# A graph layer on one core: who copies the products of picked rows, and where three steps stand in the order

## The chip, the core and the metric

The kernel runs on one core of a Trainium2 chip. The core has a matrix engine (PE; its weight loads are listed as PEld), a vector engine (DVE), a scalar engine (ACT), GpSimd (POOL), which here issues the gathers from memory, and SyncE (SP), which here issues ordinary DMAs. Each engine works through its own instruction list in order, and semaphores tie the lists together. The metric is the device time of one execution in microseconds. Three runs of the kernel before took 5995.97, 5999.37 and 6003.86 us, median 5999.37.

## The reference

One graph layer on 12500 nodes of 128 features and 412500 edges sorted by destination, then a residual sum and a layer norm:

```
f0, f1   = linear(x)                      # per node: 32 scalars, 32 three-vectors
h        = gelu(gelu(ea8 @ Wm1) @ Wm2)    # per edge, 64 wide
w00, w01, w10, w11 = h @ Wp_..            # per edge, 4 x 32 weights
mid      = products of w.., ea4 and f0[src], f1[src]
n        = segment_sum(mid, dst)          # over the edges of a node
y        = cos * self(x) + sin * linear(n)
out      = layernorm(x + y)
```

The awkward part is `f[src]`: for each of the 412500 edges a row of 128 numbers has to be brought from the node `src`, which is anywhere.

## The kernel before, in words

Edges are taken in runs of 512 (4 columns of 128 edges). Two runs are a pair, two pairs are a chunk. There are 806 runs, 403 pairs and 202 chunks. A pair with k = 0 is the first of its chunk, k = 1 the second. At the start the node features are turned and kept in SBUF (`xT`, feature by node), multiplied by `wf`, and written to a table in memory, 25 groups of up to 512 nodes.

The main loop goes over pairs `p`. The gathered rows of a pair lie in a buffer `GP[p]` (10 buffers of two runs). A column of 128 rows gets there in one of three ways:

- an indirect DMA from POOL reads 128 rows of the table (`gather`, line 223);
- 128 single-row DMAs from SP (`aid`, line 208), for one column of every fourteenth run;
- picking: ACT or DVE copies 128 single columns of `xT`, each at an address loaded into a register (`fetch`, line 174; `copy_columns`, line 188 on DVE and 192 on ACT), into a tile `gt`; when it is full, `picked_rows` multiplies it with `wf` on PE (line 197) into a PSUM tile `h`, and ACT copies the product to its place in `GP` (line 198). `SLOTS` says how many columns each engine copies at each of its places in a pair.

A column that is picked or aided needs no indirect DMA. The lists `picked` follow from `SLOTS`: with the sizes of before DVE picks 132 columns a chunk (64 and 68) and ACT 112 (56 and 56), and a product falls due wherever 128 are full; that makes 203 products on DVE, 171 on ACT, 2794 gathers. The product of a run is made two pairs before the pair that uses it.

For each pair the engines do, in this order:

- PE: `segments(p-1)` (line 670), the products of picked rows (197), `radial` (543, k = 1), `weights(p+1)` (597), `mlp1` (554, k = 0) or `mlp2` (570, k = 1) of the chunk two ahead, and at k = 0, last, `place(c-1)` (693 and 697), which moves the sums of the chunk before into a window of the bank `m`.
- ACT: `segments_kept` (676), picks, the copies of the products (198), picks, the two gelus (559 at k = 0, 576 at k = 1), each followed by picks, and at k = 0 `show` (632) between the gelus, which writes to the same bank `m`.
- DVE: at k = 0 `placing` (683) and `hot_rows` (624); then the three parts of `messages` (650, 654, 654) with picks between; at k = 1 also `select` (639), which reads what `show` wrote in the bank, and `add` (710), which adds the placed window to the sums.
- POOL: the gathers for the pair nine ahead, into the buffer that `messages(p-1)` has just finished reading.

A pick group on ACT that comes with an operation loads half of its addresses, does the operation, copies these columns, then loads and copies the other half. The PSUM tiles named `h` have two buffers, which products, `radial`, `mlp1` and `mlp2` share in the order of the program. Every eighth chunk or so a group of 512 nodes is finished: `moments` on PE, a copy and a move of the sums on ACT (741, 428), statistics on DVE.

The order is written out by hand; the framework puts in the semaphore waits. A tile's readers wait for all its writers, the bank `m` and a pair's buffer counted as one tile.

Of the kernel before, what the change touches and what calls it, by code (L numbers as in the profile page):

```python
# [8 lines left out]
F32 = mybir.dt.float32  # L9
# [3 lines left out]
AF = mybir.ActivationFunctionType  # L13
OP = mybir.AluOpType
PE = mybir.EngineType.PE
ACT = mybir.EngineType.Activation
# [5 lines left out]
P = 128  # L22
# [3 lines left out]
Q = 4  # L26
# [3 lines left out]
CH = 4  # L30
# [15 lines left out]
AID_FROM = 36  # L46
AID_LEAD = 16
STEPS = 12
SLOTS = {DVE: ((24, 20, 20), (24, 16, 28)), ACT: ((12, 16, 16, 12), (12, 16, 16, 12))}
FROM = {DVE: 6, ACT: 6}  # L50
COL_Q = {DVE: Q - 2, ACT: Q - 3}
A_OF = (1, 2, 3, 0)
# [5 lines left out]
def gnn_kernel(ctx: ExitStack, tc: tile.TileContext, x, src, dst, ea4, ea8, w1_0, w1_1, wm1, wm2,  # L58
# [120 lines left out]
    def copy_columns(e, columns):  # L179

        for at, r in columns:
# [9 lines left out]
            else:  # L191
                nc.scalar.activation(to, col, AF.Copy)  # L192

    def picked_rows(e, i):

        pt = ps.tile([P, P], F32, name="h")
        nc.tensor.matmul(pt, GT.pop((e, i)), wf, start=True, stop=True)  # L197
        nc.scalar.activation(G[picked[e][i]][:, COL_Q[e], :], pt, AF.Copy)  # L198

    def aid(s, t):  # L200

# [413 lines left out]
        nc.scalar.activation(G[s], pf, AF.Copy)  # L615

    OH = {}

    def hot_rows(c):

# [321 lines left out]
    with tc.manual_schedule(engines={PE, ACT, DVE, SP}):  # L942
        load_raw_rows(nc.sync, 0, min(3, raw_runs))
        load_w1(nc.scalar)
        if raw_runs > 3:
            load_raw_rows(nc.scalar, 3, raw_runs)
        for s in range(min(LEAD - 2, raw_runs)):
            gather(s)
        nc.vector.tensor_scalar(ident, diag, 0.0, None, op0=OP.is_equal)
        nc.vector.tensor_copy(none[:, :P], iota)  # L950
        nc.vector.tensor_copy(bank[:, 4 * SPAN:4 * SPAN + P // 2], none[:, :P].bitcast(F32))
        for b in range(min(3, NG)):
            XT[b] = load_nodes(b)
        make_wf()
        clear()
        loads = list(weight_loads())
        new_sums()
        extra = {2: lambda: load_edges(0), 3: lambda: load_attributes(0), NG // 2 - 2: lambda: turn_attributes(0), 4: lambda: load_raws(0), NG // 2: lambda: load_indices(0),
                 NG // 2 + 3: make_w1b, NG // 2 + 5: make_ws, NG - 6: lambda: radial(0), NG - 4: lambda: networks(0),
                 NG - 2: lambda: networks2(0), NG - 1: make_wpost,  # L960
                 NG // 2 + 1: lambda: nc.vector.memset(A["next"], 0.0),
                 NG - 3: run_places}
        for b in range(NG + 2):
            if b < NG:
                turn(b)
            if 0 < b <= NG:
                features_of(b - 1)
            if 1 < b:
                store_nodes(nc.scalar, table, b - 2, PF[b - 2])
            if b + 3 < NG:  # L970
                XT[b + 3] = load_nodes(b + 3)
            if b > 4 and loads:
                nc.sync.dma_start(*loads.pop(0))
            if b in extra:
                extra[b]()
        assert not loads
        for c in range(1, min(EDGES_AHEAD, NCH)):
            load_edges(c)
        if aided:
            aid_load()  # L980
        for s in range(min(LEAD - 2, raw_runs), min(LEAD, NS)):
            gather(s)
        for c in range(1, min(3, NCH)):
            radial(c)
            if c == 1:
                networks(c)
                networks2(c)
        weights(0)
        show(0)
        hot_rows(0)  # L990
        select(0)
        for s in range(PR):
            turn_rows(s)
        for s in range(PR):
            features(s)
        A["now"] = A["next"]
        clearing = []
        placed = added = 0

        def picks(e, p, i, op=None):  # L1000
            if p < FROM[e]:
                if op:
                    op()
                return
            n = SLOTS[e][p % (CH // PR)][i]
            if not op:
                copy_columns(e, fetch(e, n))
                return
            first = fetch(e, n // 8 * 4)
            op()  # L1010
            copy_columns(e, first + fetch(e, n - n // 8 * 4))

        for p in range(NP):
            c, k = divmod(p, CH // PR)
            mine = [s for s in range(p * PR, (p + 1) * PR) if s < NS]
            if p:
                for s in mine:
                    if s + LEAD - PR < NS:
                        gather(s + LEAD - PR)
            if k == 1 and c + EDGES_AHEAD < NCH:  # L1020
                load_edges(c + EDGES_AHEAD)
            for s in mine:
                if s % P == P // 2 - 16 and (s // P + 1) * P < NS:
                    load_raws(s // P + 1)
                if s % P == P // 2 and (s // P + 1) * P < NS:
                    load_indices(s // P + 1)
                if s % ET == 8 and s - 8 + ET < NS:
                    load_attributes(s // ET + 1)
                for t in range(P // ROWS):
                    a = s + AID_LEAD - t * STEPS // (P // ROWS)  # L1030
                    if a in aided:
                        aid(a, t)
            nets = c + 2 < NCH
            if k == 0:
                placing(c)
                if c + 1 < NCH:
                    hot_rows(c + 1)
            if p:
                segments(p - 1)
                picks(ACT, p, 0, lambda: segments_kept(p - 1))  # L1040
            for e in picked:
                for s in mine:
                    if (e, s + 2 * PR) in pick_of:
                        picked_rows(e, pick_of[e, s + 2 * PR])
            if k == 1 and c + 3 < NCH:
                radial(c + 3)
            cleared = bool(late)
            rest = list(kept)
            norm_kept()
            picks(ACT, p, 1)  # L1050
            if p + 1 < NP:
                weights(p + 1)
            if nets:
                (mlp1, mlp2)[k](c + 2)
                picks(ACT, p, 2, lambda: (gelu1, gelu2)[k](c + 2, 0))
            else:
                picks(ACT, p, 2)
            if k == 0 and c + 1 < NCH:
                show(c + 1)
            for s in mine:  # L1060
                if s % ET == 20 and s - 20 + ET < NS:
                    turn_attributes(s // ET + 1)
            if nets:
                picks(ACT, p, 3, lambda: (gelu1, gelu2)[k](c + 2, 1))
            else:
                picks(ACT, p, 3)
            if k == 0 and c > 0:
                place(c - 1)
                placed = c
            raws_next = [s + PR for s in mine if s + PR < raw_runs]  # L1070
            for s in raws_next:
                turn_rows(s)
            messages(p, 0)
            if k == 0:
                picks(DVE, p, 0)
            messages(p, 1)
            picks(DVE, p, 1 - k)
            for s in raws_next:
                features(s)
            if rest:  # L1080
                norm_rest()
            if cleared:
                new_sums()
                clearing += list(range(4))
            elif clearing:
                clear_sums(clearing.pop(0))
            if k == 1 and c + 1 < NCH:
                select(c + 1)
            if k == 1:
                picks(DVE, p, 1)  # L1090
            messages(p, 2)
            if k == 1 and placed > added:
                add(added)
                added += 1
            picks(DVE, p, 2)
            if k == 0 and 0 < added == c - 1:
                norm(due.get(added - 1, []))
            if p == 0:
                addresses()
                find_first()  # L1100
                new_sums()
                clearing = list(range(4))
            if p == NP - 4:
                count_odd()
        finish_waiting()
        segments(NP - 1)
        segments_kept(NP - 1)
        if late:
            norm_kept()
            new_sums()  # L1110
            clearing += list(range(4))
        norm_rest()
        finish_waiting()
        for i in clearing:
            clear_sums(i)
        for c in range(added, NCH):
            if c >= placed:
                place(c)
            add(c)
            if c < NCH - 1 and c in due:  # L1120
                norm(due[c])
                norm_kept()
                norm_rest()
                finish_waiting()
        norm_last(due[NCH - 1])
# [31 lines left out]
```

## Time and profile before

| what | value |
| --- | --- |
| median of three runs | 5999.37 us |
| profiled execution | 5962.68 us, span 5960.8 us |
| busy PE / DVE / ACT / POOL | 57% / 56% / 52% / 44% |
| granted clock of PE | 0.65 |
| indirect DMAs | 2722 from the table and 72 from x |
| column copies | 25984 on DVE (145 ns each), 21888 on ACT (189 ns each) |
| products copied by ACT | 374, 257 ns each |
| DMA | 239 MB, 40 GB/s |

Busy time counts what an engine executes; the stretch in which its sequencer loads registers, waits for semaphores or starts nothing is idle time. The column copies overlap their neighbours: a row of 16 takes 1.59 us on ACT, 20 take 1.30 us on DVE, so about 0.093 and 0.06 us each. In a timeline row the bracket at the end is the idle time of the engine just before, and who ended it; "issue" means that the profile shows no one.

### The profile page before, as it was taken

What the parts mean: (1) busy time and instruction counts of PE and PEld (TensorE: products, weight loads), DVE (VectorE), ACT (ScalarE), POOL (GpSimd) and SP (SyncE); (2) the same over time, 40 slices, a digit from 0 to 9 for tenths busy, and PEclk for the clock granted to TensorE, in tenths of its full rate; (3) what the DMA queues carried; (4) which work ended last, traced back from release to release, by engine and by line L of the source; (5) the groups of instructions that cost most, each with busy time, mean ns of one, the idle gap of its engine ahead of it and who ended that gap; (6) DMA issues with size and microseconds to landing.
All of it is one profiled execution on the core that took longest, in us unless ns stands there. A gap on an engine that the chain in (4) does not pass through costs nothing. (4 is left out here: it accounts for less than half of the span.)

```text
span 5960.8 us, 141936 instructions
## 1 busy us (share of the span) xinstructions
PE 3407.7 (57%) x30231; PEld 2603.1 (44%) x30231; DVE 3366.2 (56%) x28706; ACT 3093.4 (52%) x24111; POOL 2636.3 (44%) x2801
## 2 busy tenths in 40 slices
PE   3665655556555555555556555556655555655556
PEld 2544444444444444444444444444434444443444
DVE  1265656555655555656555665566565555665556
ACT  0254555555555555555555555555554555555554
POOL 4344444444444444444444444444444444444441
PEclk5766666666666666666666666666666666666666
DMA  4211111111111111111111111111111111111111
GB/s 100 59 36 40 39 35 38 41 35 43 42 35 39 39 37 43 40 35 36 36 41 37 40 43 38 37 40 40 41 40 35 35 38 38 40 40 34 40 33 23
DMA packets 576979, 239.04 MB, mean 40 GB/s; under 512 B 481402, under 2 KB 526570, under 8 KB 576106
## 3 DMA queue, kind: packets, MB, share of 16 engines
q0 software_dynamic: 89408, 183.29, 10.8%
q1 hardware_dynamic: 465928, 40.14, 5.4%
q10 hardware_dynamic: 20770, 6.47, 0.5%
q14 instruction: 629, 5.15, 0.3%
q8 instruction: 244, 4.00, 0.3%
HBM read 216.86 MB, written 12.99 MB: 39 GB/s over the span
## 5 line engine op out<-in xcount | busy, mean ns | idle before, releaser
L223 POOL DMA_INDIRECT G<-table,idx x2722 | 2567.2, 943 | 3208.9 <-issue 1313.3
L192 ACT ACTIVATE gt<-xT 128x1 f32 x21888 | 2329.1, 189 | 924.5 <-issue 889.3
L188 DVE COPY gt<-xT 128x1 f32 x25984 | 1891.8, 145 | 1565.0 <-issue 1520.5
L670 PE MATMUL seg<-M,S 128*32 128x128 f32 x12896 | 845.7, 371 | 444.2 <-issue 426.8
L597 PE MATMUL w<-wpb,h 64*128 64x128 f32 x6448 | 855.1, 388 | 383.7 <-issue 383.1
L597 PEld LDWEIGHTS w<-wpb,h 64*128 64x128 f32 x6448 | 699.0, 277 | 554.6 <-issue 544.1
L670 PEld LDWEIGHTS seg<-M,S 128*32 128x32 f32 x12896 | 544.3, 148 | 692.1 <-issue 643.3
L654 DVE TENSOR_TENSOR M<-w,G 128x768 f32<-128x768 f32 x806 | 761.1, 945 | 2.7 <-issue 2.7
L676 ACT ACTIVATE sg<-seg 128x256 f32<-128x256 f32 x403 | 151.1, 375 | 1112.3 <-remote 777.6
L697 PEld LDWEIGHTS m<-pl,sg 128*128 128x128 f32 x1612 | 348.6, 312 | 797.7 <-issue 797.7
L693 PE MATMUL m<-none 128*128 128x384 bf16 x202 | 90.8, 450 | 786.1 <-ACT m L632 412.6
L554 PE MATMUL h<-eT,w1b 64*128 64x128 f32 x3232 | 439.3, 403 | 125.8 <-ACT G L198 95.9
L576 ACT ACTIVATE h<-h 128x512 f32<-128x512 f32 x404 | 237.1, 589 | 491.9 <-remote 377.0
L554 PEld LDWEIGHTS h<-eT,w1b 64*128 64x128 f32 x3232 | 394.3, 303 | 159.5 <-ACT G L198 120.5
L570 PE MATMUL h<-h,w2b 64*64 64x256 f32 x3232 | 393.5, 556 | 105.7 <-ACT G L198 68.7
L197 PE MATMUL h<-wf,gt 128*128 128x128 f32 x748 | 244.0, 411 | 268.2 <-issue 154.2
L650 DVE TENSOR_TENSOR M<-w,G 128x512 f32<-128x512 f32 x403 | 275.5, 684 | 204.1 <-remote 73.9
L697 PE MATMUL m<-pl,sg 128*128 128x128 f32 x1612 | 367.5, 404 | 0.0
L197 PEld LDWEIGHTS h<-wf,gt 128*128 128x128 f32 x748 | 162.8, 263 | 403.6 <-issue 246.9
L639 DVE TENSOR_TENSOR S<-oh,m 128x512 f32<-128x512 f32 x202 | 137.2, 679 | 356.7 <-PE m L697 251.4
L559 ACT ACTIVATE h<-h 128x512 f32<-128x512 f32 x404 | 234.6, 581 | 91.0 <-remote 37.9
L570 PEld LDWEIGHTS h<-h,w2b 64*64 64x64 f32 x3232 | 187.5, 186 | 214.9 <-ACT G L198 87.3
(123 smaller groups left out, 1592.5 us busy)
## 6 DMA issues: line engine op xcount, KB each, us to landing
G<-table SPq DMA_DIRECT2D x7040, 0.5 KB
G<-table,idx POOLq DMA_INDIRECT x2722
e<-in_edge_attr SPq DMA_DIRECT2D x201, 64.0 KB
xt<-in_x SPq DMA_DIRECT2D x24, 256.0 KB
table<-ft ACTq DMA_DIRECT2D x24, 256.0 KB
xt<-in_edge_attr SPq DMA_DIRECT2D x24, 256.0 KB
out<-y SPq DMA_DIRECT2D x24, 256.0 KB
xt<-in_dst SPq DMA_DIRECT2D x5, 256.0 KB
```

Of the source, the lines that this page charges most:

```text
L188: nc.vector.tensor_copy(to, col)
L192: nc.scalar.activation(to, col, AF.Copy)
L197: nc.tensor.matmul(pt, GT.pop((e, i)), wf, start=True, stop=True)
L223: nc.gpsimd.indirect_dma_start(out=G[s][:, q, :], out_offset=None, in_=x if s < raw_runs else table, in_offset=bass.IndirectOffsetOnAxis(a ...
L554: nc.tensor.matmul(p1[h][:, j // 2, j % 2, :], w1b[rows, j, :], eT[c][rows, :], start=True, stop=True)
L570: nc.tensor.matmul(p2[r][k * HID:(k + 1) * HID, h * n:(h + 1) * n], w2b[rows, :], H1[c][h][rows, k * n:(k + 1) * n], start=True, stop=True)
L576: nc.scalar.activation(H2[c][r].rearrange("p k j e -> p (k j e)"), P2[c][r], AF.Gelu_apprx_tanh, scale=1.0 / math.sqrt(HID))
L597: nc.tensor.matmul(WP[p][:, i, q, :], H2[c][q % 2][rows, k, q // 2, :], wpb[rows, :], start=True, stop=True)
L650: nc.vector.tensor_tensor(m[:, :, :, :MUL], w[:, :, :2 * MUL].rearrange("p q (a u) -> p q a u", a=2), g[:, :, None, :MUL].to_broadcast([P, ...
L654: nc.vector.tensor_tensor(m[:, :, j, MUL:].rearrange("p q (i u) -> p q i u", i=3), w[:, :, None, (2 + j) * MUL:(3 + j) * MUL].to_broadcast ...
L670: nc.tensor.matmul(SEG[c][q * W:(q + 1) * W, r + i, :], own[:, (r + i) * Q + q, h * W:(h + 1) * W], M[p][:, i, q, h, :], start=h == 0, sto ...
L697: nc.tensor.matmul(to[:, :, bass.ds(k_at, 4 * W)].bitcast(F32), SG[c][:, k, :], PL[c][:, k, :].rearrange("p (a n) -> p a n", a=4), start=F ...
```

## The change

Five edits:

1. `SLOTS`: DVE copies 64 and 64 columns in the two pairs of a chunk (the last slot of the second goes from 28 to 24), ACT 64 and 64 (its first and last slots from 12 to 16). Every chunk then fills exactly one `gt` on each engine, with the last copy of its second pair, and both products fall due in the next pair with k = 0.
2. `picked_rows` only multiplies; a new `rows_kept` copies the product, on DVE instead of ACT, after the first part of `messages` (at k = 1 after the second).
3. `place(c-1)` stands on PE between `weights` and `mlp1`, and ahead of `show` in the program, instead of after the layer.
4. At k = 0, in nearly all chunks, DVE copies one number of each gathered row of the chunk's second pair to a small tile `landed` that nobody reads, so that it waits there for that pair's gathers.
5. The order of `messages` and the first picks is written differently; for k = 0 and k = 1 it comes out as before, but for the copies of the products.

```
-SLOTS = {DVE: ((24, 20, 20), (24, 16, 28)), ACT: ((12, 16, 16, 12), (12, 16, 16, 12))}
+SLOTS = {DVE: ((24, 20, 20), (24, 16, 24)), ACT: ((16, 16, 16, 16), (16, 16, 16, 16))}
...
+    PT = {}
+
     def picked_rows(e, i):
-        pt = ps.tile([P, P], F32, name="h")
+        PT[e, i] = pt = ps.tile([P, P], F32, name="h")
         nc.tensor.matmul(pt, GT.pop((e, i)), wf, start=True, stop=True)
-        nc.scalar.activation(G[picked[e][i]][:, COL_Q[e], :], pt, AF.Copy)
+
+    def rows_kept(e, i):
+        nc.vector.tensor_copy(G[picked[e][i]][:, COL_Q[e], :], PT.pop((e, i)))
...
+    landed = cst.tile([P, PR, Q], F32)
...
+            products = [(e, pick_of[e, s + 2 * PR]) for e in picked for s in mine if (e, s + 2 * PR) in pick_of]
+            for e, i in products:
+                picked_rows(e, i)
...
             if p + 1 < NP:
                 weights(p + 1)
+            if k == 0 and c > 0:
+                place(c - 1)
+                placed = c
             if nets:
                 (mlp1, mlp2)[k](c + 2)
...
-            if k == 0 and c > 0:
-                place(c - 1)
-                placed = c
             raws_next = [s + PR for s in mine if s + PR < raw_runs]
             for s in raws_next:
                 turn_rows(s)
+            if k == 0 and raw_runs <= PR * (p + 1) < NS - 6 * CH:
+                nc.vector.tensor_copy(landed, GP[p + 1][:, :, :, 0])
             messages(p, 0)
+            if k == 1:
+                messages(p, 1)
+            for e, i in products:
+                rows_kept(e, i)
+            picks(DVE, p, 0)
             if k == 0:
-                picks(DVE, p, 0)
-            messages(p, 1)
-            picks(DVE, p, 1 - k)
+                messages(p, 1)
+                picks(DVE, p, 1)
```

More of the change, by code (lines that the diff above doesn't have):

```diff
@@ L1040, in gnn_kernel @@
                 picks(ACT, p, 0, lambda: segments_kept(p - 1))
[L1041 to L1044, printed above, removed]
+            products = [(e, pick_of[e, s + 2 * PR]) for e in picked for s in mine if (e, s + 2 * PR) in pick_of]
+            for e, i in products:
+                picked_rows(e, i)
             if k == 1 and c + 3 < NCH:
```

## The prediction, made before the changed kernel was run

> **What bounds the kernel now.** I read the page's head and slices first, then the waits of all engines, then the order of time of single chunks, engine by engine, and last I measured intervals between named rows over 139 chunks (without the 23 in which a group of nodes is finished, and the ones after those).
>
> ```profile
> span 5960.8 us, 141936 instructions
> PE 3407.7 (57%) x30231; PEld 2603.1 (44%) x30231; DVE 3366.2 (56%) x28706; ACT 3093.4 (52%) x24111; POOL 2636.3 (44%) x2801
> ```
>
> No engine is full, and the 40 slices look alike from the fourth to the 39th, so the time is that of the chunk, 28 us, some 200 times. The list of waits says what fills the rest:
>
> ```profile
> DVE gt L188 <- issue: 1520.5, 2437, 1.7
> ACT gt L192 <- issue: 889.3, 1660, 1.2
> ACT sg L676 <- remote: 777.6, 128, 18.7
> PE m L693 <- ACT m L632: 412.6, 114, 10.9
> DVE S L639 <- PE m L697: 251.4, 69, 9.3
> DVE acc L710 <- ACT acc L428: 169.6, 15, 18.2
> ```
>
> Two things are mixed here. The first is a halt of all engines. In one chunk, on DVE and on PE:
>
> ```profile
> 3058.18 0.22 DVE L188 COPY gt<-xT 128x1 f32 x2 [1.16 <-issue]
> 3059.60 0.21 DVE L188 COPY gt<-xT 128x1 f32 x2 [1.21 <-issue]
> 3061.00 0.88 DVE L188 COPY gt<-xT 128x1 f32 x13 [1.19 <-issue]
> ...
> 3058.20 0.27 PE L670 MATMUL seg<-M,S 128*32 128x128 f32 x1 [1.12 <-issue]
> 3059.62 0.27 PE L670 MATMUL seg<-M,S 128*32 128x128 f32 x1 [1.15 <-issue]
> ```
>
> Both resume within 20 ns of each other, do one or two instructions and stop again; ACT does the same. This happens some microseconds into a burst of gathers and ends after it. Summing the stretches over 0.45 us in which no engine starts anything gives 1735 us, 0.62 us for each of 2794 gathers, and 8.5 us of a chunk. I take them out and call the rest net: 19.85 us a chunk (median).
>
> The second is a ring of real waits. The end of a chunk's first pair on PE and ACT:
>
> ```profile
> 3062.29 0.80 PE L197 MATMUL h<-wf,gt 128*128 128x128 f32 x2 [0.66 <-ACT gt L192]
> 3063.01 2.08 PE L597 MATMUL w<-wpb,h 64*128 64x128 f32 x16
> 3064.88 1.92 PE L554 MATMUL h<-eT,w1b 64*128 64x128 f32 x16
> 3070.61 0.48 PE L693 MATMUL m<-none 128*128 128x384 bf16 x1 [3.81 <-ACT h L559]
> 3072.72 1.58 PE L670 MATMUL seg<-M,S 128*32 128x128 f32 x29
> ...
> 3069.04 0.20 ACT L632 ACTIVATE m<-e 128x64 f32<-128x64 f32 x1
> 3076.05 0.38 ACT L676 ACTIVATE sg<-seg 128x256 f32<-128x256 f32 x1 [1.00 <-PE seg L670]
> ```
>
> PE has its layer done at 3066.8 and waits 3.8 us, until `show` on ACT is through, before it may place; `segments` follow, and only then ACT gets its `sg`. Net medians around this ring: show to placing 0.28, placing 1.60, segments 1.94, to sg 0.78, sg to eT 1.93, eT to gelu2 3.24, to the second gelu2 2.07, to the last column 1.52, from there to the next sg nothing (ACT is late there), sg to gelu1 3.83, to show 2.10: 19.3 of 19.85. So ACT and PE set the pace; DVE waits 1.06 us net a chunk at `select` (L639).
>
> **The change, part by part.** *Gathers.* By the sizes, 197 products on DVE and 196 on ACT, 393 for 374, so 2775 gathers for 2794: 19 halts of 0.62, **-12 us**. SP's DMAs are as many; no step moves past an SP or POOL issue.
>
> *Placing ahead.* The wait for `show` goes, and `show` now waits for the placing, which stands before `mlp1`, which ACT's gelu awaits anyway: no cost. From gelu1 to the next sg ACT no longer passes through PE: two gelus with their picks, 2.27, and 2.24 to the last column, for 2.10 + 0.28 + 1.60 + 1.94 + 0.78 = 6.70. Four more columns in the last slot are 4 x 0.093 = 0.37, sum 4.88: **-1.82 us a chunk**. The 1.60 us of placing turn up elsewhere, next.
>
> *128 columns a pair of slots, on ACT.* The last copy of the second pair now always fills `gt`, and PE's product waits for it. This already occurs in every eighth chunk, and the rows above (3062.29) show it: PE waits for the last column, then product, weights, layer, gelu1. In these 20 chunks the time is 28.59 us (+-0.39) against 27.27 in the 56 others with an ACT product at k = 0. Next to it, the placing now stands in this stretch. Its length: last column to weights 0.78, weights 1.87, placing 1.60, layer to gelu1 2.13 (lower quartile, where PE is the later), sum 6.38; ACT took 0.09 less than 3.83 = 3.74 for it. **+2.64 a chunk.** In the second pair: eight columns more +0.74, in its first and last slot; products' copies gone from there, 0.9 a chunk x 0.37 with their waits, -0.33; eT to gelu2 shorter since PE gets its layer earlier, between 0 and -0.78 (its lower quartile is 2.46), I take -0.39. **+0.02.** Sum of the ring: -1.82 + 2.64 + 0.02 = +0.84 us.
>
> *Copies of products on DVE.* The nearest row is another copy of this shape out of PSUM:
>
> ```profile
> L479 DVE COPY colv<-h 128x128 f32<-128x128 f32 x6 | 1.8, 292 | 5.4 <-PE h L478 3.7 <-issue 1.7
> ```
>
> Two a chunk, 0.6 us. The waits for semaphores before them lie behind the 0.68 us of L650. Behind a copy that waits for PE are queued the register loads of 24 picks. Do they run ahead? After a wait at L710:
>
> ```profile
> 3175.49 0.56 DVE L710 TENSOR_TENSOR acc<-m,acc 128x384 f32 x1 [18.20 <-ACT acc L428]
> 3177.44 1.79 DVE L188 COPY gt<-xT 128x1 f32 x28 [1.39 <-issue]
> ```
>
> The load begins in the trace 0.01 us after L710, not during the 18 us before: it stays behind a waiting instruction, and 1.39 us lie bare; up to 1.35 here. [...] DVE's own ring: 19.85 less 1.06 (`select` no longer waits) less 0.26 (waits at L650) less 0.24 (four columns) plus 0.6 plus 0.1 for `landed` is 18.99; with the load bare 20.3. Both ends are kept; below 20.69, ACT's ring, DVE just waits, as PE's product ends a median 4.7 us after L650 even now. If ACT's ring became shorter than this, DVE's would decide.
>
> *The small read.* Its gathers were issued eight pairs before, over 100 us; what it waits for has landed. It moves some semaphore checks from the columns ahead of L650 at k = 1, where copies go on at 0.06 to 0.1 us each, behind the 0.28 us of L624. Between -0.3 and +0.2 a chunk, 0.1 taken, counted above. PE's layer needs both `h` buffers, held until DVE has copied; weights and placing (3.47 us) cover that as long as DVE isn't later than PE by more.
>
> *Chunks that finish nodes.* They take 37.8 us against 27.7. Their `moments` stand behind the placing, so what PE waits for `show` goes there too, and segments, the sums' move (L428) and DVE's L710 come earlier. Between 0 and 4 us (placing and the wait for it), taken 2.6 x 23 = **-60 us**; 0 and -92 are the ends.
>
> *Sum:* 198 x 0.84 = +166, -12, -60: **+94 us** on 5962.68, the profiled execution, which lies 0.6% under the median of the runs, 5999.37. On the median: **6093 us**.
>
> **The rivals.** *DVE's ring decides (faster).* If the ACT-PE stretch is hidden, by layer and placing running while ACT still copies or by gelu1 not being what comes last, the chunk falls to 18.99, -0.86: 198 x -0.86 - 12 = -182, 5817 us. For it: the wait of PE at L693 (786 us in all with its other releasers) and of DVE at L639 both vanish, and chunks with both products at k = 0 take 26.7 us against 27.7 for all without node groups. Against: a new wait of PE for ACT's last column, visible above. It decides if the ACT-PE stretch costs less than +1.0 instead of +2.64.
>
> *The two rings couple (much slower).* DVE waits for the product, its late segments then keep PE, and both wait in turn. The eighth chunks, with the product waiting for the last column, show net 20.9 against 19.15 for their siblings, +1.76: 198 x 1.76 - 12 = +336, 6335 us.
>
> *Nothing measurable:* gain and new wait cancel, 0 +- 12 us, 5999. Under 0.2%, 12 us, this kernel can't be told from no change.
>
> **How the numbers follow.** Forecast (ring longer by 0.45 to 1.23 us a chunk) 0.45, coupled rings 0.15, DVE's ring 0.33, cancelled 0.07. Slower 0.60, same 0.07, faster 0.33. The likeliest case alone, with its ends (0.39 more or less a chunk at gelu2, 0 to -92 at the node groups), is 5984 to 6231. The range, with the cases of both signs: 5800 to 6260.
>
> **What would show it.** In the profile after: L693 waits no longer for L632 or L559, and L639 not for L697 (right: placing ahead). L197 waits for ACT's `gt` in nearly each chunk, some 200 times instead of 25, and L559 waits for L554 (right: the new stretch). The copy of the product on DVE has idle time before it, released by PE, of 1 us or more a chunk, and the columns after it start over 1 us later. If instead L559 has no wait and the product's copy none either, the forecast is wrong and DVE's ring sets the time. Halts should stay near 1720 us; if they change by more than 100, that is a cause that I did not count.

## The result and the profile after

The changed kernel takes 6356.31 us (median of 4, 6343.62 to 6358.80), the kernel before 5997.67 us beside it (median of 4). The ratio is 1.060, 95% interval 1.057 to 1.063: **358 us slower** (358.64). The prediction had the direction; its number, 6093 us, and its range up to 6260 were too low. The profiled execution took 6357.74 us, 395 more than the one of before.

The head of the page of the changed kernel:

```profile
span 6356.0 us, 142999 instructions
PE 3159.0 (50%) x30269; PEld 2291.1 (36%) x30269; DVE 3304.2 (52%) x28520; ACT 3371.6 (53%) x26937; POOL 2619.9 (41%) x2782
```

ACT has 278 us more to do and DVE 62 less, as the sizes say. PE's recorded time fell from 3407.7 to 3159.0 us with nearly the same number of matmuls (30231 and 30269). No engine is near full: the 395 us are waiting. The list of waits of all engines, changed kernel:

```profile
PEld h L575 <- ACT eT L550: 1347.4, 193, 9.1
DVE G L203 <- remote: 1220.4, 148, 10.0
ACT sg L682 <- remote: 946.4, 213, 16.5
PE h L199 <- ACT gt L192: 790.0, 165, 8.2
ACT h L564 <- PE h L559: 445.9, 194, 5.3
DVE G L203 <- PE h L199: 340.4, 222, 8.7
DVE acc L716 <- ACT acc L433: 44.5, 17, 3.5
```

The waits that should go are gone: placing for `show` (L693 before, now L699) and `select` for placing (L639, now L645) have 6.7 and 27.9 us of idle time left in all, and L710 (now L716) fell from 169.6 to 44.5 us. The waits that should come are there: the product waits for ACT's last column 165 times, gelu1 for the layer 194 times. PE's layer of the second pair (L575) now waits 1251 us for ACT's `eT` (1347 in the row of its weight loads), where it waited 31 before; `eT` stands behind `sg` on ACT, so this can be the delay of `sg` passed on, but no run takes it apart. The largest new wait is that of DVE's copy, 1560 us, and 1220 of it have the releaser "remote". That word stands where a semaphore event released the instruction and the trace has no instruction that ended at that event: either the work waited for had ended earlier and the news of it came later, or its record is missing. In the rows below the record is there. They show one such place, on DVE, then PE, then ACT:

```profile
3205.63 0.68 DVE L656 TENSOR_TENSOR M<-w,G 128x512 f32<-128x512 f32 x1
3214.06 0.29 DVE L203 COPY G<-h 128x128 f32<-128x128 f32 x1 [7.75 <-remote]
3214.90 0.29 DVE L203 COPY G<-h 128x128 f32<-128x128 f32 x1 [0.56 <-PE h L199]
3216.69 1.55 DVE L188 COPY gt<-xT 128x1 f32 x24 [1.50 <-issue]
...
3207.27 0.27 PE L199 MATMUL h<-wf,gt 128*128 128x128 f32 x1 [0.24 <-issue]
3214.07 0.79 PE L199 MATMUL h<-wf,gt 128*128 128x128 f32 x2 [6.54 <-ACT gt L192]
...
3212.23 0.20 ACT L192 ACTIVATE gt<-xT 128x1 f32 x1 [1.14 <-issue]
3212.93 0.20 ACT L192 ACTIVATE gt<-xT 128x1 f32 x1 [0.50 <-issue]
3213.63 0.39 ACT L192 ACTIVATE gt<-xT 128x1 f32 x3 [0.49 <-issue]
3214.01 0.38 ACT L682 ACTIVATE sg<-seg 128x256 f32<-128x256 f32 x1
```

POOL issued eight gathers from 3202.27 to 3211.00. From 3207.5 the core goes in halts: ACT copies one or two columns every 0.70 or 1.40 us. PE's first product was done at 3207.54, yet the copy of it on DVE starts at 3214.06, with the halt's end; within 60 ns of it ACT gets `sg` and PE its second product. The trace has the updates of PE's semaphore for the segments (ended at 3205.76) and for the first product at 3213.99 and 3214.03. PE's second product is no such case: ACT's last column itself ended at 3214.02. In between neither DVE nor PE did anything. In the kernel before both used these steps for columns and segment matmuls (the rows at 3058 to 3061 in the prediction). Counted over the whole traces: in the stretches made of halts that follow each other within 0.45 us and last over 1 us together, PE starts about 1000 matmuls before and about 480 after, although the stretches are some 500 us longer in all after.

By the prediction's own measure, stretches over 0.45 us in which no engine starts anything:

| | before | after |
| --- | --- | --- |
| profiled execution | 5962.7 | 6357.7 |
| halts | 1735 | 2146 |
| halts per gather | 0.62 | 0.77 |
| time less halts | 4228 | 4212 |

The whole loss stands in the halts. A wait that lies in a halted stretch counts as halt here, so this says where the time is lost, not yet what loses it. Longer bursts don't explain it. The changed kernel has mostly bursts of six and eight gathers where the kernel before has mostly seven, but at the same length the halts rose: from 2.5 to 4.4 us in a burst of six, 4.2 to 4.7 in one of seven, 5.2 to 6.0 in one of eight. With the values of before, the new lengths would give no more halts than the old ones.

### The profile page after: what moved, and what is told of

Read it like the earlier page. It is cut to its first block, busy times and chain, and to the rows that moved or that the text cites. A ratio compares the mean times of both kernels' runs of the same rounds, so it can differ in the third digit from the quotient of the medians.

```text
span 6356.0 us, 142999 instructions
## 1 busy us (share of the span) xinstructions
PE 3159.0 (50%) x30269; PEld 2291.1 (36%) x30269; DVE 3304.2 (52%) x28520; ACT 3371.6 (53%) x26937; POOL 2619.9 (41%) x2782
## 5 line engine op out<-in xcount | busy, mean ns | idle before, releaser
L192 ACT ACTIVATE gt<-xT 128x1 f32 x25088 | 2645.0, 189 | 965.2 <-issue 929.7
L188 DVE COPY gt<-xT 128x1 f32 x25216 | 1748.2, 145 | 1039.5 <-issue 1028.7
L575 PE MATMUL h<-h,w2b 64*64 64x256 f32 x3232 | 521.5, 604 | 1273.3 <-ACT eT L550 1251.0
L203 DVE COPY G<-h 128x128 f32<-128x128 f32 x393 | 113.3, 291 | 1578.0 <-remote 1220.4
L676 PE MATMUL seg<-M,S 128*32 128x128 f32 x12896 | 722.3, 346 | 382.2 <-DVE M L660 196.3
L602 PE MATMUL w<-wpb,h 64*128 64x128 f32 x6448 | 715.8, 377 | 50.0 <-issue 49.5
L575 PEld LDWEIGHTS h<-h,w2b 64*64 64x64 f32 x3232 | 196.2, 199 | 1475.1 <-ACT eT L550 1347.4
L676 PEld LDWEIGHTS seg<-M,S 128*32 128x32 f32 x12896 | 455.2, 137 | 636.8 <-issue 341.7
L602 PEld LDWEIGHTS w<-wpb,h 64*128 64x128 f32 x6448 | 601.7, 270 | 132.3 <-issue 112.7
L559 PE MATMUL h<-eT,w1b 64*128 64x128 f32 x3232 | 283.3, 324 | 10.0 <-ACT eT L550 10.0
L559 PEld LDWEIGHTS h<-eT,w1b 64*128 64x128 f32 x3232 | 244.2, 228 | 46.1 <-issue 25.6
L645 DVE TENSOR_TENSOR S<-oh,m 128x512 f32<-128x512 f32 x202 | 135.1, 669 | 27.9 <-issue 26.9
```

What stands on the lines that cost most here:

```text
L188: nc.vector.tensor_copy(to, col)
L559: nc.tensor.matmul(p1[h][:, j // 2, j % 2, :], w1b[rows, j, :], eT[c][rows, :], start=True, stop=True)
L575: nc.tensor.matmul(p2[r][k * HID:(k + 1) * HID, h * n:(h + 1) * n], w2b[rows, :], H1[c][h][rows, k * n:(k + 1) * n], start=True, stop=True)
L602: nc.tensor.matmul(WP[p][:, i, q, :], H2[c][q % 2][rows, k, q // 2, :], wpb[rows, :], start=True, stop=True)
L676: nc.tensor.matmul(SEG[c][q * W:(q + 1) * W, r + i, :], own[:, (r + i) * Q + q, h * W:(h + 1) * W], M[p][:, i, q, h, :], start=h == 0, sto ...
```

## The experiments

Two theories from this. **The longer ring** (A): last column, product, copy and register load lie on the ring of waits and make it longer, halts or not. **Held handoffs** (B): within the stretch in which a burst of gathers halts the core, an engine still does its own ready work in steps of 0.7 us, but what it gets from another engine comes only when the burst is over; so each new handoff near a burst costs what is left of the stretch. A third (C): the gathers halt the core more for a reason of their own. The runs were made in groups, each on one chip, with the kernel before beside them; that took 5981 to 6054 us in four groups (a fifth, at the end, differs), so ratios are compared, and times only within a group.

### Nearly no gathers, and single parts undone

The cut, in both kernels (the buffers of the gathered rows are then kept, not allocated anew):

```
+            if 0 < q and 40 * PR <= s < NS - 1:
+                continue
```

> The kernel before, but from pair 40 on only the first column of each run is gathered (two indirect DMAs a pair instead of six to eight); the other gathered columns keep old rows, so the output is not the layer's. Everything else is issued as before. All theories: the halts nearly go, since bursts of four or fewer gathers show 0.1 to 0.85 us of halts in the trace of before; what is left is the time net of halts, 5998 - 1700 = about 4300 us. It is the base for the next run.

> The changed kernel with the same cut (two indirect DMAs a pair from pair 40 on, old rows in the other gathered columns). Theory A, the ring of real waits is longer even without halts: slower than the cut kernel before by the prediction's 0.84 us a chunk (+166 us) up to the 1.76 of its coupled case (+350 us). Theory B, the longer ring costs only where it meets the halts, since waiting engines make no use of the steps that a halt leaves them: within 60 us of the cut kernel before. Theory C, the gathers halt the core more for a reason of their own: the same as B here, and told from it by the runs that undo single edits.

Measured: 4206.28 us (ratio 0.703, 0.6996 to 0.7063) and 4365.96 us (0.7296, 0.7262 to 0.7330). Halts are 346 and 332 us, and the base is 94 us lower than expected. The whole change costs **160 us** without bursts, near the prediction's +166 for the ring. So A is right for that part, and about 200 of the 358 us need the gathers that the cut takes away. The two cut kernels are not the full ones less their halts alone: PE's granted clock is 0.76 in both, against 0.65 and 0.67. The same place in the cut changed kernel, DVE then PE:

```profile
2002.55 0.29 DVE L203 COPY G<-h 128x128 f32<-128x128 f32 x1 [1.80 <-PE h L199]
2004.30 1.54 DVE L188 COPY gt<-xT 128x1 f32 x24 [1.45 <-issue]
...
2002.03 0.49 PE L199 MATMUL h<-wf,gt 128*128 128x128 f32 x2 [2.00 <-ACT gt L192]
```

The copy starts 0.03 us after the product's end, where it took 6.5 us above. The register load behind it is bare in both (1.45 and 1.50 us), as the prediction had it.

Products made one pair later, when `gt` has long been full:

```
-products = [... pick_of[e, s + 2 * PR] ...]
+products = [... pick_of[e, s + PR] ...]
```

> The changed kernel with the products made one pair later (one pair before their use instead of two, so in the second pair of a chunk), where gt has been full for a whole pair. Theory B (and A): PE's product no longer waits for ACT's last column, DVE's copy no longer for PE's product, and the time falls to between the prediction's case of DVE's own ring, 5817 us, and 6100 us. Theory C (halts of their own): within 100 us of 6356.

Measured: 6273.61 us, ratio 1.0487 (1.0449 to 1.0525). By the ratios that is only 68 us better than the change. The wait for the last column is gone (1.3 us are left), but it wasn't the main thing:

```profile
ACT sg L682 <- remote: 1894.7, 320, 15.7
DVE G L203 <- remote: 975.6, 167, 6.5
PEld h L548 <- DVE G L203: 881.2, 169, 7.9
```

The copy still waits 6 us at a time for a product that PE has finished, and now `radial` waits for the buffer that it holds. This speaks against a chain that begins with the last column, and for handoffs that are held at their new place too.

Copies back on ACT, right behind the product, with all else changed:

```
             for e, i in products:
                 picked_rows(e, i)
+                nc.scalar.activation(G[picked[e][i]][:, COL_Q[e], :], PT.pop((e, i)), AF.Copy)
...
-            for e, i in products:
-                rows_kept(e, i)
```

> The changed kernel with the products copied by ACT right after the matmul, as before; sizes, placing ahead and the small read stay. If DVE's place in the chain (last column on ACT, product on PE, copy on DVE, and the register load behind it) is what costs, 6000 to 6150 us; if the sizes alone do (the product waits for the last column whoever copies it), 6200 to 6360 us, or above, since ACT now waits for PE itself.

Measured: 6190.41 us, ratio 1.0348 (1.0310 to 1.0387): between the two cases. By the ratios DVE's copies are worth some 150 us of the 358; the rest stays.

### Each edit alone

The new `SLOTS` alone; `place(c - 1)` between `weights` and the layer alone; `rows_kept` on DVE alone with the old sizes; and the change without `landed`.

> The kernel before with the new sizes alone. ACT still copies the products, the placing stays behind the layer. By the prediction's terms (+2.64 a chunk without the 1.60 of the placing, +0.02, 198 chunks, -12): 5990 + 198 = about 6190 us. If the sizes do nothing but set when a product falls due, and the order of ACT hides it: 5970 to 6010. The run with ACT's copies in the changed kernel gave 6190, so if this one gives the same, placing ahead and the small read are worth nothing together.

> The kernel before with the placing ahead of the layer alone. By the prediction's terms: -1.82 a chunk, of which the 1.60 of the placing can turn up ahead of the layer, and -60 at the node groups: 5880 to 5990 us with 5930 as its middle (5570 if nothing turned up elsewhere). Rival: the placing, which had been done while ACT is between its gelus, now holds the layer back in the stretch in which the gathers halt the core: 6050 us or more.

> The changed kernel without the small read. By the prediction (-0.3 to +0.2 us a chunk): 6315 to 6420 us, and near 6340. Rival: the read makes DVE wait at the chunk's head for a burst that is still under way, or fixes the place of the halts in the chunk: 6250 or less.

> The kernel before with the products copied by DVE alone (at the changed kernel's place in its order); the old sizes, the placing behind the layer, no small read. If DVE's copy is what costs, through its wait for PE and the register load behind it: 6100 us or more even here. If it costs only together with sizes that make both products wait for the last column: 5960 to 6060.

| edit | time, us | ratio to before | interval |
| --- | --- | --- | --- |
| sizes alone | 6234.68 | 1.0426 | 1.0381 to 1.0471 |
| placing ahead alone | 5923.30 | 0.9894 | 0.9853 to 0.9935 |
| copies on DVE alone | 6419.83 | 1.0724 | 1.0681 to 1.0767 |
| change without small read | 6351.19 | 1.0615 | 1.0572 to 1.0658 |

The kernel before took 5990.65 us beside them. Placing ahead is a gain, 67 us. The small read is nothing beyond the intervals. The sizes cost 244 us, where 198 were expected. And **DVE's copies, priced at nearly nothing, cost 429 us**, more than the whole change. The three add up to 606 us, the change has 358: they are not independent.

The copies on DVE show the held handoff most plainly. PE, then POOL's last gather, ACT and DVE, in that kernel:

```profile
3008.99 1.94 PE L676 MATMUL seg<-M,S 128*32 128x128 f32 x32
3010.86 0.80 PE L199 MATMUL h<-wf,gt 128*128 128x128 f32 x2
...
3016.00 0.37 PE L602 MATMUL w<-wpb,h 64*128 64x128 f32 x1 [1.03 <-issue]
3016.73 0.37 PE L602 MATMUL w<-wpb,h 64*128 64x128 f32 x1 [0.36 <-issue]
...
3016.22 0.94 POOL L228 DMA_INDIRECT G<-table,idx  x1 [0.30 <-issue]
...
3019.03 0.38 ACT L682 ACTIVATE sg<-seg 128x256 f32<-128x256 f32 x1 [10.58 <-remote]
...
3019.07 0.29 DVE L203 COPY G<-h 128x128 f32<-128x128 f32 x1 [9.12 <-remote]
```

Segments are done at 3010.9 and both products at 3011.7. PE goes on with its own weights, one matmul every 0.70 to 1.40 us from 3014.62 on. ACT's `sg` and DVE's copy start 40 ns apart, at 3019.05, some 8 and 7 us late; the trace has updates of PE's semaphore at 3019.01, 3019.05 and 3019.09 and none from 3009 to then. In this kernel both engines that wait for PE stand still through the burst. Counted over whole traces, the next update of PE's semaphore comes over 4 us after the recorded end of the instruction that makes it 438 times of 2566 in the kernel before, 789 of 2431 in this one and 825 of 2585 in the changed kernel, but 57 and 55 times in the two cut kernels (133 of the 2566 updates of the kernel before and 76 of the 2585 of the changed one have no record, so these counts are rather too high). The waits of this kernel, and the same kernel's with two gathers a pair (next part):

```profile
ACT sg L682 <- remote: 2020.7, 258, 12.6
DVE G L203 <- remote: 1260.5, 209, 9.4
```

```profile
ACT sg L685 <- remote: 237.1, 60, 10.1
DVE G L203 <- remote: 86.4, 16, 7.9
```

In the kernel before, `sg` waited so for 777.6 us and the gelus of L576 for 377.0, but the copies of the products, then on ACT, for only 0.3. So handoffs were late before the change too; the change put more of them there. The sizes' cost has its own mark in their kernel, the wait for the last column:

```profile
PE h L197 <- ACT gt L192: 650.5, 176, 8.3
```

### Pauses that did not stand where they were written

To shorten the bursts, POOL was given small iota tiles between the gathers of a pair.

```
+        if s >= 40 * PR and s % PR == 0:
+            for _ in range(12):
+                nc.gpsimd.iota(pause, pattern=[[1, 128]], base=0, channel_multiplier=0)
```

> The kernel before with the gathers of a pair in two halves: from pair 40 on POOL writes twelve small iota tiles (some 3 us by the 0.23 us of the two iotas in the trace of before) after the gathers of the pair's first run. Theory D, halts and held handoffs belong to long bursts (bursts of four show at most 0.85 us of halts, bursts of eight 5.3): at most 4 x 0.85 = 3.4 us of halts a chunk instead of 8.5, so 4600 to 5200 us. Rival, halts follow the number of gathers, however they are spaced (0.62 us each): 5950 to 6050 us.

> The changed kernel with the gathers of a pair in the same two halves. Theory D (what the change lost beyond the 160 us of its longer ring are handoffs between engines held until a burst is over): within 100 to 220 us of the kernel before in halves. Rival (the loss has nothing to do with the bursts): the loss of 358 us stays.

> The kernel before with the placing ahead of the layer (5923 us alone) and the gathers in two halves. If both gains hold side by side: 60 us less than the kernel before in halves. If the placing's gain came from the bursts alone: the same as it.

> The kernel before with two of these iotas after every gather, so that a gather takes about 1.75 us instead of 1.25 and a burst of seven 12 us of the pair's 14. If the halts come from gathers that follow each other too fast: halts near zero and 4400 to 5000 us. If a halted stretch begins 3.5 us after the first gather and ends with the last one whatever their spacing: longer stretches, 6200 us or more.

Measured: 7019.37, 7358.61, 6955.37 and 7162.42 us (ratios 1.159, 1.216, 1.150 and 1.184). They don't test what they were made for. The iota tiles depend on nothing, and the framework's own ordering put them early: in the trace all 4356 of them (5012 in the last) ran before 1841 us (2098), about a hundred at a time ahead of a pair's gathers, and after that the gathers stand in the same bursts as ever. They delayed the first part (1022 us of iota in the first of these traces), and that is all. What can be read is that the change still costs 339 us beside them and the placing still gains 64.

### Each edit with two gathers a pair, and bursts cut in two

The same cut as above, on the three single edits. And, with all gathers, a pause that holds: a copy on POOL that reads from the first run's last gathered column and writes to the second run's buffer.

```
+        if s >= 40 * PR and s % PR == 1:
+            last = 0 if s - 1 in aided else Q - 1
+            nc.gpsimd.tensor_copy(G[s][:, :, :1], G[s - 1][:, last:last + 1, :1].to_broadcast([P, Q, 1]))
```

> The kernel before with the products copied by DVE (+429 us with all gathers), but with two indirect DMAs a pair from pair 40 on (old rows in the other gathered columns, so the output is not the layer's). If the handoff from PE to DVE is dear because a burst holds it: within 60 us of the cut kernel before (4206 us). If DVE's wait and the register load behind it are a longer ring by themselves: 4206 + 300 to 430 us. In between, the share of each is read off.

> The kernel before with the new sizes (+244 us with all gathers), with the same cut. A longer ring by the prediction's terms (last column, product, weights, layer): 4206 + 210 = about 4420 us. If the wait for the last column is dear because of the bursts: below 4270.

> The kernel before with the placing ahead of the layer (-67 us with all gathers), with the same cut. A shorter ring: 4206 - 40 to - 100 us. If its gain lies in how the order meets the bursts: within 30 us of 4206.

> The kernel before with every pair's gathers in two bursts of three or four: ahead of the second run's gathers POOL copies four numbers a row from the first run's last gathered column to the second run's buffer (which its gathers then overwrite), so that it waits for that landing; from pair 40 on. It takes the place of the runs with iota tiles, whose pauses did not stand between the gathers. If long bursts make the halts (a burst of four shows at most 0.85 us, one of eight 5.3): at most 3.4 us of halts a chunk for 8.5, 4900 to 5400 us. If halts go with the number of gathers: 5950 to 6100 us. If a halted stretch lasts from the first gather to the last landing whatever lies between: longer than before, 6100 us or more.

Here the kernel before took 6054.14 us, in the group of the cut kernel before 5981.51. The cut kernel before was not run again on this chip, so the first three differences are rough; they are given by times and by ratios (times 6000 us).

| edit | all gathers | two a pair, by times | by ratios |
| --- | --- | --- | --- |
| sizes | +244 | 4494.79, +289 | +238 |
| placing ahead | -67 | 3919.03, -287 | -333 |
| copies on DVE | +429 | 4427.56, +221 | +171 |
| the whole change | +358 | 4365.96, +160 | +160 |

The sizes cost about the same with and without bursts: that is the longer ring, somewhat dearer than the 210 us expected. DVE's copies cost half or less without bursts; in their full kernel the time less halts grew by 171 us (4228 to 4399) and the halts by 286 (1735 to 2021), which is much the same division. And the placing's gain is **four to five times as large** without bursts, which neither case expected; with them the time less halts fell by 216 us (to 4012), and the halts took back 177 (1912).

The split bursts, with all gathers: **5693.31 us, ratio 0.9412 (0.9380 to 0.9444)**, 361 us faster than the kernel before beside it. POOL in that kernel:

```profile
2999.14 0.94 POOL L226 DMA_INDIRECT G<-table,idx  x1 [0.30 <-issue]
3001.64 0.19 POOL L218 COPY G<-G 128x4 f32<-128x4 f32 x1 [1.55 <-DMA G<-table,idx]
3002.10 0.98 POOL L226 DMA_INDIRECT G<-table,idx  x1 [0.27 <-POOL G L218]
```

Halts fell from 1735 to 1356 us with the same 2794 gathers: they follow the length of the burst, not the number of gathers alone. By length, in this trace: 0.76 us in a burst of three, 1.65 of four, 4.76 of seven, 6.04 of eight. The expectation had 0.85 for four, and 5400 us at most; the direction was right, the gain smaller. One reason is that not all bursts were cut: where POOL was late, a pair's first half followed directly on the second half of the pair before, and the 118 bursts of six or more gathers that are left from pair 40 on hold some 590 of the 1356 us.

### Split bursts with the edits

> Placing ahead of the layer and the gathers of a pair in two bursts, otherwise the kernel before; both gained alone (ratios 0.989 and 0.941 to the kernel before). If the long bursts ate the placing's gain (287 us with two gathers a pair, 67 with all): more than the product of the two, ratio 0.89 to 0.92. If the two are independent: 0.931. If the split bursts still hold the layer's new place: 0.94.

> The changed kernel with the gathers of a pair in two bursts. If what the change lost beyond its longer ring (160 us with two gathers a pair) is the bursts' doing: 100 to 220 us above the kernel before in two bursts (ratio 0.958 to 0.978 to the kernel before). If it is not: 358 us above it (ratio 1.000).

Measured: 4317.57 us (ratio 1.1136, 1.1100 to 1.1171) and 4276.76 us (1.1037, 1.0996 to 1.1078), beside a kernel before that took **3876.40 us** (3865.93 to 3888.58, 7 runs). This group was on a chip on which the kernel before runs 2100 us faster than on the others. In the two traces the halts are 280 and 213 us, 0.10 and 0.08 per gather, though the bursts have six to eight, and no wait of any engine has the releaser "remote". The kernel before itself has no trace from this chip. There POOL is the limit of the split kernels: copy to copy, one pair, in the kernel with the placing ahead:

```profile
2507.72 0.19 POOL L218 COPY G<-G 128x4 f32<-128x4 f32 x1 [1.67 <-DMA G<-table,idx]
2508.18 0.97 POOL L226 DMA_INDIRECT G<-table,idx  x1 [0.27 <-POOL G L218]
...
2518.25 0.19 POOL L218 COPY G<-G 128x4 f32<-128x4 f32 x1 [1.62 <-DMA G<-table,idx]
```

This pair takes 10.53 us: seven gathers of 1.25 us and 1.78 for the wait and the copy. The 363 split pairs take 10.59 us on the average, some 3840 of its 4316 us. So these two runs do not answer their question, and the two edits can't be compared in them. Whether the change gains or loses on such a chip was not measured.

## Why the prediction was wrong, point by point

**Direction: right, and for one of its reasons.** The ring with the last column is longer, as it said: for the sizes alone +198 by its terms, 244 measured (289 or 238 without bursts). That the whole change costs 160 us with the bursts taken away, where the sum had +166 for the ring, is in part luck. By single edits the sum had +198 for the sizes, about -44 for the placing (198 x (-1.82 + 1.60)) and nothing for DVE's copies; without bursts they measure about +240 to +290, -290 to -330 and +170 to +220. Errors of opposite sign cancel.

**The failing step** is "I take them out and call the rest net". The sum was made of net times, with halts added as 0.62 us by the number of gathers. The step fails in both halves. Halts follow how long a burst is (0.76 us for three gathers, 6.04 for eight), and at the same length they rose with the change, while PE found only half as many matmuls to start in these stretches. And a wait for another engine inside a stretch isn't a net wait of 1 or 2 us: in the rows shown it lasts to the stretch's end, 6.5 to 8 us. The halts, with the waits that lie in them, rose by 411 us where -12 stood. The text had named this as a sign: a change by more than 100 is "a cause that I did not count".

**Copies on DVE: the mis-sized term.** It had 0.6 us a chunk for the copies and up to 1.35 for the bare load, hidden as long as DVE's ring is below ACT's. They cost 171 to 221 us without bursts (about 1 us a chunk) and 429 with them (2.2 a chunk). The load is bare, 1.50 us in the changed kernel's row, as the row of before said (1.39 us). What was not hidden is the handoff from PE to DVE: 148 of the 393 copies waited for late news, 1220 us in all. ACT's copies in the kernel before had no such wait (4.3 us of idle time before all 374).

**Placing ahead: right in what it removes, and right in size only by the halts.** The waits vanished as said. Alone it is 5923 us; 5930 was on record as the middle of a range, while the sum's own terms, -44 and -60, give some 5890. But without bursts it is worth 287 to 333 us, close to the 1.82 us a chunk (360 us) that the ring's terms gave before the 1.60 of the placing was charged again. So the 1.60 (317 us) does not come back as such; with bursts, the halts take back 177 us.

**Node groups: taken -60 us.** Their 23 chunks fell from 37.83 to 35.71 us, but the ones after them rose from 23.35 to 28.70. The two together rose by 3.2 us where two other chunks rose by 4.3 (28.2 to 30.4 each), so about 1 us of each, some 25 us, can be a gain. **Small read: nothing** beyond the intervals (ratios 1.0600 with it, 1.0615 without), as said.

**The rivals.** "The two rings couple" gave 6335 us and 6356 was measured. Its picture is in part what the trace shows: DVE waits for the product (1560 us), PE for DVE's late segments only 196 us (4 before). Its price, 1.76 us of net time a chunk from the eighth chunks, does not stand behind the number, since the time less halts is unchanged. That it came within 21 us is luck. "DVE's ring decides" falls: the copy's wait and the register load it needed to be hidden are both there.

**Open.** Why a burst halts PE, DVE and ACT (POOL goes on with a gather every 1.25 us), and why signals between engines are late in it, no run shows; nor is theory C, more halts for a reason of their own, excluded as a part of the loss. PE's own weights went on while the updates of its semaphore were missing for 8 us, which fits news that is held and not work that is held; but the ends of matmuls are modelled in the profile, so this is argued, not shown. That the consumers start late is shown. In the cut kernel 0.03 us lie between the product's recorded end and DVE's copy of it; whether the 6.5 to 8 us inside a burst are the same delay, made longer, the traces don't show.

## What to carry to other kernels

When a trace shows all engines halting during bursts of indirect gathers, don't subtract the halts and plan with the rest: look for handoffs between engines that fall in the burst. To keep there only work that each engine has ready by itself follows from this, but no run here did it; the one that moved the products by a pair gained 1%. Price a new handoff by its place, and test it with the bursts taken away; here that separated the longer ring (160 us) from what needs the bursts (about 200) in one pair of runs. A data dependence that breaks a burst of eight in two halves was worth more (6%, in the kernel before) than placing ahead (1%), on a chip that halts; on the one that hardly does (0.08 to 0.10 us a gather), the same dependence in two other versions made POOL the limit, so measure on the chip that counts.

## What was not expected of the hardware

- Halts are not a constant of a gather: 0.25 us of each in bursts of three, 0.41 in fours, 0.76 in eights, in the kernel with split bursts.
- In two halted stretches ACT and DVE started 6.5 to 8 us after the recorded end of the PE instruction they waited for, about 3 us after the last gather was issued, and within 50 ns of each other.
- One chip had nearly none of this: 0.08 to 0.10 us of halts per gather in the two split kernels, whose bursts have six to eight, and 3876 us for the kernel before, which takes about 6000 on the others.
